# Graph attention on one core: feature transposes first in TensorE's turn, q[dst]·k last on VectorE, logits transposed one step earlier

## The chip, the cores and the metric

The kernel runs on one core of one Trainium2 chip. The metric is device time in microseconds (us), from start to end of one launch; the median over runs counts, and lower is better. Engines: PE (TensorE), DVE (VectorE), ACT (ScalarE), POOL (GpSimd), SP (SyncE, which issues most DMAs).

## The reference

One layer of graph attention over N = 12500 nodes and E = 212500 edges, sorted by destination, with 128 features in 8 heads of 16:

```python
h = jnp.maximum(_layernorm(x, axis=-1), 0.0)
q = (h @ Wq.T + bq).reshape(N, 8, 16)
k = (edge_attr @ Wk.T + bk).reshape(-1, 8, 16)
v = (h @ Wv.T + bv).reshape(N, 8, 16)
qs, qd = q[src], q[dst]
in_m   = sum(qs * k, -1)
out_m  = sum(qd * k, -1)
diag_m = sum(qs * qd, -1)
score = (segment_softmax(in_m * SCALE, dst) + segment_softmax(out_m * SCALE, dst)
         + segment_softmax(diag_m * SCALE, dst)) * distance ** lam
out = segment_sum(score[..., None] * v[dst], dst).reshape(N, 128) @ Wo.T + bo
return x + leaky_relu(out, 0.1)
```

So each edge needs three products of rows (q[src]·k, q[dst]·k, q[src]·q[dst]), each summed within 8 heads: 24 logits an edge, then a softmax over the edges of a node.

## The kernel before

**Steps and turns.** The edges lie in 415 blocks of 512 (4 columns of 128 edges). A block is a step g of the loop at L1586. Five steps (s = 0 to 4) make a turn t; there are 83 turns. The five blocks of a turn lie far apart in the list, so that their scans run side by side on 120 partitions (5 blocks × 24 logits).

**What a step does**, in the order in which the loop's body issues it:

- `gather(g + 18)` (L683): four indirect DMAs by POOL fetch q[src] for a block 18 steps ahead into one of 20 buffers `qq`.
- `spread_q(g + 1)`: four matmuls in bf16 (L1229) turn a window of q rows (`win`) and one-hot columns (`oh`) into q[dst], in PSUM `qd_ps` (2 buffers); ACT copies it to SBUF `qd` (L1232, 2 buffers).
- `project(g + 1)`: a bias matmul (L1219) and four fp32 matmuls (L1221, eight records in the trace) make k from the transposed features `eT`, in PSUM `k_ps` (2 buffers).
- `turn(g + 2)`: four transposes (L1212) of the edge features `ea` into PSUM `eT_ps` (one buffer); ACT copies that to `eT` (L1214, 3 buffers).
- `logits(g)`: DVE makes three products into `prod` (one buffer): qd·k (L1240), qq·qd_ps (L1241), qq·k (L1242), and reduces them by heads (L1243) into `lT`.
- `one_hots(g + 3)`: ACT makes the columns `oh` (L1206, L1207).

**What a turn does besides**, by its step s, for turns whose logits are complete:

- s = 0: `turn_logits(t - 2)` transposes `lT` into PSUM `l_ps` (L1263), `turn_head(t - 1)` transposes the next turn's first 64 edges into `h_ps` (L1271); DVE scans `l_ps` forwards in place (L1303) and copies its last column (`carry`, L1306), then scans the head (L1311, L1314).
- s = 1: DVE scans back (L1333) to the maximum of each node.
- s = 2: `turn_max` transposes the maxima (`m_ps`, L1345); DVE subtracts (L1353), ACT takes the exponential (L1354).
- s = 3: `show_ends` makes selection matrices on PE (`d_ps`, L1379) and ACT (`sel`, L1382, L1383); DVE weighs (L1365).
- s = 4: `to_rows` sums the edges into rows of nodes on PE (`w_ps`, L1393); ACT copies them (L1398), SP stores them.

These small PSUM tiles (`l_ps`, `h_ps`, `m_ps`, `d_ps`, `w_ps` and those of the node work mixed in) share three buffers.

**What sets the order.** Every engine runs its instructions in the order in which the code issues them: `pin` chains each instruction to the one before it on its engine, so an instruction that waits holds up all behind it. Between engines, semaphores follow the data. One order more is written out: `behind[g + 1, j]` names the PE instruction issued last at four points of a step, and the j-th gather of the next step's `gather` waits for it, besides waiting for its buffer `qq` to be free and for the gather before it:

```python
                if (g - LOOK, j) in behind:
                    tc.add_manual_dep(rows.ins, behind[g - LOOK, j], mybir.DependencyInfo(
                        mybir.DependencyClass.Sync, mybir.DependencyReason.SCHED_ONLY),
                        reason="close behind the products")
```

So PE's order in a step is: spread, project, transposes, then the small product of that s; the four gathers of the next step are opened by these four, in this order. PE's waits before: the spread for DVE's L1241 two steps back (it frees `qd_ps`), the bias for L1242 two steps back (it frees `k_ps`), the k product for ACT's copy `eT` of its own block. The transposes wait for nothing that the product before them hasn't waited for.

Of the kernel before, what the change touches and what calls it, by code (L numbers as in the profile page):

```python
# [472 lines left out]
def ordered_path(ctx: ExitStack, tc: tile.TileContext, flag, x, src, dst, edge_attr, edge_weight,  # L473
# [19 lines left out]
    nc = tc.nc  # L493
# [9 lines left out]
    G = T - 1  # L503
# [51 lines left out]
    pinned = {}  # L555

    def pin(inst):

        engine = str(inst.ins.engine)
        if engine in pinned:  # L560
            tc.add_manual_dep(inst.ins, pinned[engine], mybir.DependencyInfo(
                mybir.DependencyClass.NoSync, mybir.DependencyReason.DATA), reason="in order")
        pinned[engine] = inst.ins.name
        return inst
# [57 lines left out]
    end = S * G  # L622
# [11 lines left out]
    qqs, st, eas, behind, base_v = {}, {}, {}, {}, {}  # L634
# [33 lines left out]
    def fetch_edges(t):  # L668
        if t < G:
            ea = eas[t] = load.tile([P, S, JN * F], F32, name="ea")  # L670
            pin(nc.sync.dma_start(
                ea, edge_attr[:end * BE, :].rearrange("(s b p j) f -> p s b (j f)", s=S, b=G, p=P)
                [:, :, t, :]))
# [3 lines left out]
    def gather(g):  # L677
        if g < end:
            qq = firsts[g] if g < FIRST else gath.tile([P, JN, F], F32, name="qq")
            s, t = g % S, g // S  # L680
            for j in range(JN):
                of, at = (x, raw["i"][t]) if g < RAW else (q_table, src_i)
                rows = pin(nc.gpsimd.indirect_dma_start(  # L683
                    out=qq[:, j, :], out_offset=None, in_=of,
                    in_offset=bass.IndirectOffsetOnAxis(
                        ap=at[:, s, j:j + 1] if g < RAW else at[:, s * G + t, j:j + 1], axis=0)))
# [4 lines that stand above are left out]
            qqs[g] = qq  # L691
# [32 lines left out]
    with tc.tile_pool(name="prep", bufs=1) as prep, \  # L724
# [294 lines left out]
        for g in range(RAW):  # L1019
            turn = 1 + 2 * g if g < 4 else GN + g - 5  # L1020
# [81 lines left out]
    class Nodes:  # L1102
# [39 lines left out]
        def turn(self, to):  # L1142
            for b in range(self.n):
                pin(nc.tensor.transpose(to[:, b, :], self.h[:, b, :], ident))
            if self.hT is None:
                self.hT = fin.tile([P, JN, P], F32, name="hT")
            pin(nc.scalar.copy(self.hT[:, :self.n], to[:, :self.n]))
# [48 lines left out]
    with tc.tile_pool(name="work", bufs=2) as work, \  # L1196
            tc.tile_pool(name="scan", bufs=2) as scan, \
            tc.tile_pool(name="ps", bufs=1, space=PSUM) as ps:
        ks, eTs, qds, q_ps, ohs, lTs = {}, {}, {}, {}, {}, {}

        def one_hots(g):

            if g < end:
                oh = ohs[g] = work.tile([K3, BE], BF, name="oh", bufs=5)
                d = st[g // S]["relb"][:, g % S, :]
                pin(nc.scalar.activation(d, d, AF.Abs, bias=before[:K3]))  # L1206
                pin(nc.scalar.activation(oh, d, AF.Relu, bias=1.0, scale=-1.0))  # L1207
# [9 lines left out]
        def project(g):  # L1217
            k_ps = ks[g] = ps.tile([P, JN, F], F32, name="k_ps", bufs=2)
            pin(nc.tensor.matmul(k_ps, ones3, bk3, start=True, stop=False))  # L1219
            for j in range(JN):  # L1220
                pin(nc.tensor.matmul(k_ps[:, j, :], eTs[g][:, j, :], wk, start=False,  # L1221
                                     stop=(j == JN - 1)))
            del eTs[g]

        def spread_q(g):
            s, d = g % S, st[g // S]
            qd_ps = q_ps[g] = ps.tile([P, JN, F], F32, name="qd_ps", bufs=2)
            for j in range(JN):
                pin(nc.tensor.matmul(qd_ps[:, j, :], ohs[g][:, j * P:(j + 1) * P],  # L1229
                                     d["win"][:, s, :], start=(j == 0), stop=(j == JN - 1)))  # L1230
            qds[g] = work.tile([P, JN, F], F32, name="qd")
            pin(nc.scalar.copy(qds[g], qd_ps))  # L1232
            del ohs[g]

        def logits(g):
            s, t = g % S, g // S
            if s == 0:
                lTs[t] = scan.tile([P, JN, S, H3], F32, name="lT", bufs=4)
            prod = work.tile([P, JN, 3, F], F32, name="prod", bufs=1)
            pin(nc.vector.tensor_mul(prod[:, :, 2, :], qds[g], ks[g]))  # L1240
            pin(nc.vector.tensor_mul(prod[:, :, 1, :], qqs[g], q_ps[g]))  # L1241
            pin(nc.vector.tensor_mul(prod[:, :, 0, :], qqs[g], ks[g]))  # L1242
            pin(nc.vector.tensor_reduce(lTs[t][:, :, s, :],  # L1243
                                        prod.rearrange("p j i (h d) -> p j (i h) d", d=DIM), AX.X,
                                        ALU.add))
            del ks[g], qds[g], q_ps[g], qqs[g]
# [121 lines left out]
        def select(t):  # L1368
            at, part = block_rows(t)
            ends = ends_t[t % 2 if t < G - 1 else t - G + 3]  # L1370
            pin(nc.sync.dma_start(ends[1:, :], rel_d[part].rearrange("(s b) (j p) -> s b j p", b=G, j=JN)
                                  [:, at, :, :]))
# [42 lines left out]
        def later(f, t, *more):  # L1415
            if 0 <= t < T:
                f(t, *more)

        def nodes_before(t, s):

            new, old = pairs.get(t - t % 2), pairs.get(t - t % 2 - 2)
            if new and t % 2 == 1 and s == 4:
                new.project_v(small([P, JN, F], "node_ps"))
            if old and t % 2 == 0 and s == 4:
                old.project_o(small([P, JN, F], "node_ps"))
# [155 lines left out]
        products = str(mybir.EngineType.PE)  # L1581
# [9 lines left out]
        for g in range(end):  # L1591
            s, t = g % S, g // S
            nodes_before(t, s)
            if g >= FIRST:
                gather(g + LOOK)
            if s == 0:
                fetch_edges(t + 1)
            if g + 1 < end:
                spread_q(g + 1)
                behind[g + 1, 0] = pinned[products]  # L1600
                project(g + 1)
                behind[g + 1, 1] = pinned[products]
            if g + 2 < end:
                turn(g + 2)
                behind[g + 1, 2] = pinned[products]
            logits(g)
            one_hots(g + 3)
            if s == 0:
                later(turn_logits, t - 2)
                later(turn_head, t - 1)  # L1610
                later(scan_here, t - 2)
                if t > 1:
                    scan_head(t - 1)
                later(select, t - 2)
            elif s == 1:
                later(scan_back, t - 2)
                if t == 1:
                    logits_few()
            elif s == 2:
                later(turn_max, t - 2)  # L1620
                later(powers, t - 2)
                if t == G - 1:
                    turn_logits(t - 1)
                    scan_on(t - 1)
            elif s == 3:
                later(show_ends, t - 2)
                later(weigh_powers, t - 2)
                fetch(t + 2)
            else:
                later(to_rows, t - 2)  # L1630
            ahead, k = (t + 2, s - 3) if s > 2 else (t + 1, s + 2)
            if ahead > 1:
                fetch_rows(ahead, [k])
            later(put_rows, t - 2 if s == 4 else t - 3, [(s + 1) % S])
            if t == G - 1:
                if 0 < s < 4:
                    select(G - 3 + s)
                elif s == 4:
                    for i in (G - 2, G - 1, G):
                        show_ends(i)  # L1640
            behind[g + 1, 3] = pinned[products]
            nodes_between(t, s)
            terms_between(t, s)
            if g == 4:
                show_places()
            elif g == 7:
                show()
            elif 0 <= g - 21 < len(tests):
                tests[g - 21]()
            begin_rest(g - (end - DRAIN))  # L1650
            if g < S:
                of = [u for u in range(NU) if g in parts_of(u)]
                pin(nc.scalar.dma_start(
                    sums[g][of[0] * UN:(of[0] + len(of)) * UN].rearrange(
                        "(n p) i c -> p n (i c)", p=P),
                    blank[:, None, :].to_broadcast([P, 2 * len(of), 2 * 2 * H3])))
# [97 lines left out]
```

## Time and profile before

| | |
|---|---|
| median of 3 runs | 2754.93 us (2752.01 to 2763.2) |
| profiled execution | 2753.89 us |
| its span, first to last instruction | 2752.0 us |
| granted TensorE clock, mean | 0.763 |
| DMA, read and written | 320.86 MB, 32.17 MB |
| loop in its steady part, 300 to 2580 us | 379 reduces, 1516 gathers |
| busy there | PE 1589.71, DVE 1773.01, ACT 1145.24, POOL 1440.12 us |

How to read the lines of groups: line of code, engine, operation, output<-inputs, shapes, count | busy us in all, mean ns of one | idle us of that engine just before them, and what ended most of it. "remote" and "issue" stand for waits whose releaser the profile doesn't name. In a timeline the first two numbers are the start and the duration, and a bracket holds the idle time ahead and its releaser. PE's groups of matmuls are shown as one row each, and their ends are modelled.

### The profile page before, as it was taken

What the parts mean: (1) busy time and instruction counts of PE and PEld (TensorE: products, weight loads), DVE (VectorE), ACT (ScalarE), POOL (GpSimd) and SP (SyncE); (2) the same over time, 40 slices, a digit from 0 to 9 for tenths busy, and PEclk for the clock granted to TensorE, in tenths of its full rate; (3) what the DMA queues carried; (4) which work ended last, traced back from release to release, by engine and by line L of the source; (5) the groups of instructions that cost most, each with busy time, mean ns of one, the idle gap of its engine ahead of it and who ended that gap; (6) DMA issues with size and microseconds to landing.
All of it is one profiled execution on the core that took longest, in us unless ns stands there. A gap on an engine that the chain in (4) does not pass through costs nothing.

```text
span 2752.0 us, 36272 instructions
## 1 busy us (share of the span) xinstructions
PE 1869.1 (68%) x10744; PEld 1495.9 (54%) x10744; DVE 2061.8 (75%) x2844; ACT 1370.8 (50%) x2518; POOL 1595.9 (58%) x1683
## 2 busy tenths in 40 slices
PE   2736666666677767666767767676667776776786
PEld 1624555555555655555556556555555565655664
DVE  3636787777787877877878777777877778778894
ACT  2734545444455545554555445455444554555572
POOL 6244666666666666666666666666666666666400
PEclk9867777877777778788787777777877777777786
DMA  6247444444454454444434444444444444344321
GB/s 185 84 135 219 119 134 121 133 136 125 127 153 140 124 151 135 128 149 124 125 121 138 128 121 121 140 127 121 123 136 120 118 143 134 110 137 130 116 88 51
DMA packets 321411, 355.65 MB, mean 129 GB/s; under 512 B 135266, under 2 KB 241005, under 8 KB 320896
## 3 DMA queue, kind: packets, MB, share of 16 engines
q1 hardware_dynamic: 250853, 237.91, 27.3%
q0 software_dynamic: 53184, 108.92, 15.7%
q10 hardware_dynamic: 17168, 6.41, 1.0%
q8 instruction: 88, 1.44, 0.2%
q14 instruction: 118, 0.97, 0.1%
HBM read 320.86 MB, written 32.17 MB: 128 GB/s over the span
## 4 chain that ended last, share of the span: by engine, by line
PE 37%; DVE 18%; ACT 15%; another core or an unknown queue 14%; issue 13%; DMA 1%; SPq 1%; ACTq 1%; DVEq 0%; POOL 0%; POOLq 0%
PE k_ps L1221 12%; PE w_ps L1393 7%; PE eT_ps L1212 5%; DVE lT L1243 4%; PE qd_ps L1229 4%; ACT eT L1214 3%; PE k_ps L1219 3%; DVE prod L1240 2%; DVE prod L1241 2%; DVE l_ps L1303 2%; ACT relb L1206 2%; ACT oh L1207 2%; DVE prod L1242 2%; ACT qd L1232 2%
## 5 line engine op out<-in xcount | busy, mean ns | idle before, releaser
L683 POOL DMA_INDIRECT qq<-q_table,src_i x1608 | 1528.9, 951 | 940.0 <-issue 323.3
L1221 PE MATMUL k_ps<-wk,eT 128*128 128x128 f32 x3320 | 655.9, 358 | 508.2 <-issue 261.5
L1221 PEld LDWEIGHTS k_ps<-wk,eT 128*128 128x128 f32 x3320 | 555.9, 253 | 661.9 <-issue 356.8
L1243 DVE TENSOR_REDUCE lT<-prod 128x96 f32<-128x1536 f32 x415 | 727.5, 1753 | 14.4
L1214 ACT COPY eT<-eT_ps 128x512 f32<-128x512 f32 x415 | 244.4, 589 | 785.1 <-remote 539.4
L1240 DVE TENSOR_TENSOR prod<-qd,k_ps 128x512 f32<-128x512 f32 x415 | 281.1, 677 | 197.1 <-remote 134.2
L1232 ACT COPY qd<-qd_ps 128x512 f32<-128x512 f32 x415 | 240.7, 580 | 229.5 <-PE qd_ps L1229 72.7
L1212 PE MATMUL eT_ps<-ident,ea 128*128 128x128 f32 x1660 | 342.8, 345 | 0.9 <-DVE qq L992 0.9
L1229 PE MATMUL qd_ps<-win,oh 126*128 126x128 bf16 x1660 | 186.5, 243 | 171.0 <-DVE prod L1241 82.6
L1206 ACT ACTIVATE relb<-relb,before 126x512 bf16<-126x512 bf16 x415 | 302.4, 729 | 0.0
L1242 DVE TENSOR_TENSOR prod<-qq,k_ps 128x512 f32<-128x512 f32 x412 | 280.3, 680 | 0.0
L1241 DVE TENSOR_TENSOR prod<-qq,qd_ps 128x512 f32<-128x512 f32 x412 | 280.1, 680 | 0.0
L1212 PEld LDWEIGHTS eT_ps<-ident,ea 128*128 128x128 f32 x1660 | 276.0, 185 | 1.1 <-DVE qq L992 1.1
L1207 ACT ACTIVATE oh<-relb 126x512 bf16<-126x512 bf16 x415 | 262.1, 632 | 15.3 <-DMA q_table<-q3o 2.2
L1229 PEld LDWEIGHTS <-oh 126*128 126x128 bf16 x1660 | 139.4, 110 | 230.3 <-issue 215.9
L1393 PE MATMUL w_ps<-back,sel 128*126 128x144 f32 (+1 forms) x1344 | 239.9, 343 | 25.5 <-ACT sel L1383 6.3
L1393 PEld LDWEIGHTS w_ps<-back,sel 128*126 128x126 f32 (+1 forms) x1344 | 222.0, 238 | 52.6 <-ACT sel L1383 34.7
L1303 DVE TENSOR_TENSOR_SCAN l_ps<-far,carry,l_ps 120x512 f32<-120x512 bf16 x80 | 103.0, 1288 | 187.4 <-remote 65.0
L1219 PE MATMUL k_ps<-b,ones 3*128 3x512 bf16 x415 | 178.5, 430 | 18.6 <-DVE prod L1242 11.2
L1333 DVE TENSOR_TENSOR_SCAN m<-far,head,l_ps 120x512 f32<-120x512 bf16 x81 | 103.0, 1272 | 0.0
L1398 ACT COPY rows<-w_ps 126x288 f32<-126x288 f32 x84 | 33.1, 395 | 134.1 <-PE l_ps L1263 35.1
L1353 DVE TENSOR_TENSOR back<-lT,m_ps 128x480 f32<-128x480 f32 x83 | 54.1, 652 | 54.0 <-PE m_ps L1345 16.2
(230 smaller groups left out, 1697.4 us busy)
## 6 DMA issues: line engine op xcount, KB each, us to landing
ea<-in_edge_attr_dram SPq DMA_DIRECT2D x83, 1280.0 KB
relb<-rel_d SPq DMA_DIRECT2D x83, 630.0 KB
qq<-q_table,src_i POOLq DMA_INDIRECT x1608
win<-q_table SPq DMA_DIRECT2D x415, 31.5 KB
far<-far_d SPq DMA_DIRECT2D x84, 120.2 KB
q_table<-q SPq DMA_DIRECT2D x18, 384.0 KB
sums<-rows SPq DMA_DIRECT2D x412, 7.9 KB
q_table<-xq SPq DMA_DIRECT2D x24, 256.0 KB
```

The lines of the kernel that those rows point to most:

```text
L683: rows = pin(nc.gpsimd.indirect_dma_start(out=qq[:, j, :], out_offset=None, in_=of, in_offset=bass.IndirectOffsetOnAxis(ap=at[:, s, j:j + ...
L1206: pin(nc.scalar.activation(d, d, AF.Abs, bias=before[:K3]))
L1207: pin(nc.scalar.activation(oh, d, AF.Relu, bias=1.0, scale=-1.0))
L1212: pin(nc.tensor.transpose(eT_ps[:, j, :], eas[g // S][:, g % S, j * F:(j + 1) * F], ident))
L1214: pin(nc.scalar.copy(eT, eT_ps))
L1221: pin(nc.tensor.matmul(k_ps[:, j, :], eTs[g][:, j, :], wk, start=False, stop=(j == JN - 1)))
L1229: pin(nc.tensor.matmul(qd_ps[:, j, :], ohs[g][:, j * P:(j + 1) * P], d["win"][:, s, :], start=(j == 0), stop=(j == JN - 1)))
L1240: pin(nc.vector.tensor_mul(prod[:, :, 2, :], qds[g], ks[g]))
L1241: pin(nc.vector.tensor_mul(prod[:, :, 1, :], qqs[g], q_ps[g]))
L1242: pin(nc.vector.tensor_mul(prod[:, :, 0, :], qqs[g], ks[g]))
L1243: pin(nc.vector.tensor_reduce(lTs[t][:, :, s, :], prod.rearrange("p j i (h d) -> p j (i h) d", d=DIM), AX.X, ALU.add))
L1393: pin(nc.tensor.matmul(w_ps[:, i].rearrange("p s c -> p (s c)"), d["sel"][:n, j, lo:lo + 3, :].rearrange("p s w -> p (s w)"), d["back"][:n ...
```

## The change

Three things move; no instruction is added or taken away on any engine.

1. In the loop, `turn(g + 2)` goes ahead of `spread_q(g + 1)` and `project(g + 1)`. The points that open the gathers are renamed in the new order: the first gather of the next step follows the transposes, the second the spread, the third the project, the fourth the small product, as before.
2. In `logits`, the product of q[dst] and k (into `prod[:, :, 2]`) moves from first to last; qq·q[dst] is now first and qq·k second.
3. `turn_logits` of a turn moves from step s = 0 to the step before it, s = 4 of the turn before, behind `to_rows`.

PE's order in a step is then: transposes, spread, project, small product. The transposes of g + 2 now come before the k product of g + 1, and wait for ACT's copy of the transposes of g + 1, since `eT_ps` has one buffer; the k product has no wait of its own left. The spread waits for DVE's first product two steps back, as it is the one that reads `qd_ps`. DVE's first product needs `qd_ps` and `qq`, the second `k_ps`, the third ACT's copy `qd`. The small PSUM tiles are handed out in the same order as before.

```diff
@@ logits
             prod = work.tile([P, JN, 3, F], F32, name="prod", bufs=1)
-            pin(nc.vector.tensor_mul(prod[:, :, 2, :], qds[g], ks[g]))
             pin(nc.vector.tensor_mul(prod[:, :, 1, :], qqs[g], q_ps[g]))
             pin(nc.vector.tensor_mul(prod[:, :, 0, :], qqs[g], ks[g]))
+            pin(nc.vector.tensor_mul(prod[:, :, 2, :], qds[g], ks[g]))
@@ the loop
+            if g + 2 < end:
+                turn(g + 2)
+                behind[g + 1, 0] = pinned[products]
             if g + 1 < end:
                 spread_q(g + 1)
-                behind[g + 1, 0] = pinned[products]
+                behind[g + 1, 1] = pinned[products]
                 project(g + 1)
-                behind[g + 1, 1] = pinned[products]
-            if g + 2 < end:
-                turn(g + 2)
                 behind[g + 1, 2] = pinned[products]
             logits(g)
             one_hots(g + 3)
             if s == 0:
-                later(turn_logits, t - 2)
                 later(turn_head, t - 1)
...
             else:
                 later(to_rows, t - 2)
+                if t < G - 1:
+                    later(turn_logits, t - 1)
```

## The prediction

> **What bounds the kernel now.** I read the page's totals first, then the groups of lines over the steady loop (300 to 2580 us), the waits there, one timeline, and the groups again over 2610 to 2680 us, where no gathers run.
>
> ```profile
> PE 1869.1 (68%) x10744; PEld 1495.9 (54%) x10744; DVE 2061.8 (75%) x2844; ACT 1370.8 (50%) x2518; POOL 1595.9 (58%) x1683
> ...
> PE 37%; DVE 18%; ACT 15%; another core or an unknown queue 14%; issue 13%; DMA 1%; SPq 1%; ACTq 1%; DVEq 0%; POOL 0%; POOLq 0%
> ```
>
> No engine is full, and 27% of the chain is waits without a named owner (14% + 13%). The loop shows where they sit:
>
> ```profile
> L683 POOL DMA_INDIRECT qq<-q_table,src_i x1516 | 1441.2, 951 | 840.0 <-issue 301.1 <-remote 244.7 <-PE qd_ps L1229 80.4
> L1243 DVE TENSOR_REDUCE lT<-prod 128x96 f32<-128x1536 f32 x379 | 664.4, 1753 | 13.1
> L1221 PE MATMUL k_ps<-wk,eT 128*128 128x128 f32 x3032 | 600.7, 359 | 487.6 <-issue 257.9 <-ACT eT L1214 227.4 <-ACT qd L1232 1.8
> ...
> L1214 ACT COPY eT<-eT_ps 128x512 f32<-128x512 f32 x378 | 222.7, 589 | 744.9 <-remote 529.2 <-PE qd_ps L1229 115.4 <-PE eT_ps L1212 62.8
> ...
> L1229 PE MATMUL qd_ps<-win,oh 126*128 126x128 bf16 x1516 | 170.0, 243 | 154.6 <-DVE prod L1241 76.1 <-issue 43.6 <-DVE prod L1240 25.0
> ...
> L1303 DVE TENSOR_TENSOR_SCAN l_ps<-far,carry,l_ps 120x512 f32<-120x512 bf16 x76 | 97.9, 1288 | 186.7 <-remote 65.0 <-PE qd_ps L1229 29.6 <-PE h_ps L1271 26.9
> ```
>
> 379 reduces in 2280 us make 6.02 us a step, though DVE needs 1773.0 us there and PE 1589.7. Next to PE's own work, its largest idle time is 487.6 us ahead of the product with k, for ACT's copy of eT; and that copy stood 744.9 us, 529.2 of them behind nothing named. The timeline shows why:
>
> ```profile
> 1509.00 0.60 PE L1212 MATMUL eT_ps<-ident,ea 128*128 128x128 f32 x4
> ...
> 1513.08 0.38 PE L1229 MATMUL qd_ps<-win,oh 126*128 126x128 bf16 x4 [3.04 <-DVE prod L1241]
> ...
> 1515.68 0.59 ACT L1214 COPY eT<-eT_ps 128x512 f32<-128x512 f32 x1 [5.32 <-remote]
> ...
> 1516.32 2.07 PE L1221 MATMUL k_ps<-wk,eT 128*128 128x128 f32 x8 [2.27 <-issue]
> ```
>
> The transposes end at 1509.60; the idle ACT copies 6.08 us later, 1.66 us after POOL's gather that ran from 1513.07 to 1514.02. PE's word reaches ACT late, often only in POOL's pauses. Without gathers the same lines read:
>
> ```profile
> L1243 DVE TENSOR_REDUCE lT<-prod 128x96 f32<-128x1536 f32 x15 | 26.3, 1753 | 0.5
> L1221 PE MATMUL k_ps<-wk,eT 128*128 128x128 f32 x112 | 19.6, 328 | 0.1
> ```
>
> 15 reduces in 70 us are 4.67 us a step, and PE's wait is 0.1. So two things set the pace together: POOL's gathers (0.95 busy + 0.30 between = 1.25 us; 1516 take 1895 of the 2280 us, leaving 385 us of pauses, of which I counted 258 over 0.5 us, so 5.9 gathers a run), and PE, whose progress opens the gathers and which stands for late copies.
>
> **The change part by part.** (a) Work: the same instructions on every engine; 0 us. SP's queue keeps its order. POOL issues the same gathers; their four gates, before spread, project, transposes, small product, are now transposes, spread, project, small product. In a circle that is PE's same order, so they open at the same spacing: 0 us. The first gather of a step also waits for the last product that reads its old buffer; this is now the second instead of the third, 0.60 us earlier, counted under (d).
>
> (b) Slack for eT. Before, between transposes of g+1 and their use lie the small product, the spread (170.0/379 = 0.45 us) and the bias (162.9/379 = 0.43). Now the k product (600.7/379 = 1.58) lies between as well, so each stall ahead of k can shrink by up to 1.58. Counted in the loop's timeline: 185 stalls, of which 1.58 or less each gives 243.5 us (130 are longer and keep a rest). That is PE time, not the end's. Two ways to carry it over: PE spends 1589.7/1516 = 1.05 us on each gather's share, so a pause filled with 243.5/258 = 0.94 us more PE work opens about 0.9 gathers, runs grow from 5.9 to 6.8, the pause of 1.49 us (385/258) is spread over more, and a gather costs 1.25 + 1.49/6.8 = 1.469 us instead of 1.503: 1516 × 0.034 = 51 us. Or from the loop itself: over 70 turns I regressed a turn's length on its stalls; a us of k stall costs 0.34 us, one of qd stall 0.58. 243.5 × 0.34 = 82. I take the middle, **-66**; bounds 0 (POOL's runs unchanged) and -243.
>
> (c) The new wait. Transposes of g+2 now wait for the copy of g+1, as eT_ps is one buffer, and spread, project and small queue behind them; DVE and the gathers wait for these. Cover is 0.45 + 0.43 + 1.58 = 2.46 us plus the small product, against a copy of 0.589 plus the lateness; where it suffices, 0. Where a late word comes at POOL's pause whatever PE did, k now follows by transposes (313.8/379 = 0.83), spread and bias: 1.71 us later than before. If that holds for all 130 long stalls: 130 × 1.71 × 0.34 = 76. I take a quarter, as a run usually ends when PE's gates are exhausted, so moves with PE: **+19**; bounds 0 and 76.
>
> The Trainium skill ("Perfetto Trace Analysis", Optimizing Tensor Performance, Matmuls) wants independent matmul groups rotated through PSUM banks so that one's evacuation overlaps the next's matmuls; this single eT_ps, refilled at the head of the turn, speaks against the change. By the rule each step would pay the copy, 0.589 × 415 = 244 us more; by the rows above other products lie between. No run here shows it yet.
>
> (d) Order of the products. qq·q[dst] goes first (needs no k and no copy of q[dst]); it frees qd_ps 0.60 us earlier (start to start, timeline). 78 qd stalls, the first 0.6 of each: 48 us × 0.58 = 28 at most; k becomes first need of the second product, and DVE's 176.8 us ahead of its first product moves there or shrinks. The q[dst] copy is freed 1.2 us later, under the reduce of 1.753; if that cover is gone, ACT's copy is late, and eT's copy, queued behind it, with it. I take **-10**; bounds -28 and, for the copy, at 78 stalls (1.2 less the spread's 0.45) × 0.34 = +20.
>
> (e) l_ps one step earlier. The scan's 186.7 us over 76 turns moves to the head scan, which still needs h_ps; only the scan and carry, 1.288 + 0.16 = 1.45 us a turn, can run before that: counted, 96.9 us, at 0.13 us per us (same regression, scan wait) = 13. PE's l_ps is the same 46.4 us, now in s=4 behind w_ps, where a gather gate moves 0.61 us later. **-4**; bounds -13 and +8 (76 × 0.61 × 0.17, half the k rate).
>
> Sum: -66 + 19 - 10 - 4 = -61. The profiled execution took 2753.89 us (span 2752.0 and 1.9 around it), 1.0 under the median of 2754.93. 2755 - 61 = **2694**.
>
> **The clock.** PE's clock falls after stalls: the k product takes 1.16 us at 1508.01 and 2.07 at 1516.32; the loop's mean is 0.76, and 0.85 without gathers. Fewer stalls could raise it; I count it in the low bound only. The skill's "TensorE: Matmul & The Clock Gate", Why this matters for your kernels, says gaps over about 3 us throw the clock back to half, and this row's 2.27 us stall behind a 3.04 one fits; by it, shortening the 130 longest stalls under 3 us would give back some of the 0.9 us each.
>
> **Rivals.** 1. *Larger gain* (15%): the lateness follows PE, nearly all of the 243.5 lands on runs of 8 gathers or more: 1.25 + 1.49/8 = 1.436 us, -101, and half of the loop's clock loss on k (0.9 us × 130 / 2 × 0.34 = 20), so 2634. For: 4.67 us a step is possible. Against: POOL's 1895 us remain.
> 2. *No change* (13%): a run is what PE opened since the last pause, and each pause lets one copy of eT through, so PE gets one set of transposes further, in either order; runs stay 5.9, (b) and (c) are 0, and half of (d) and (e), which hang on PE's word too, gives -7: 2748. For: copies bunch 1.5 to 2.2 us after a run's last gather. Against: one step opens 4 gathers, and most runs have 5 to 8.
> 3. *Slower* (25%): the blocked transposes. The word comes at POOL's pause, so all 185 stalls stay as long, and k follows each by 1.71: 185 × 1.71 × 0.34 = +108, less 20 for (d) and (e): 2843. Between it and (b) it decides from 243.5/1.71 = 142 of 185 stalls that are fixed by POOL; at 160 of them, (160 - 142) × 1.71 × 0.34 = +10. Middle of this case 2800. For: the shown copy came with the pause. Against: the median lateness of PE's word, which I counted at 2.2 to 2.7 us, is inside the new cover.
>
> **How the numbers follow.** The forecast has 47%; with rival 1 that is 0.62 for faster by over 0.5% (14 us, about what a measurement can tell from no change), 0.13 within, 0.25 slower. The forecast's own range is 2655 to 2735 ((b) from -51 to -82, (c) from 0 to 76, the others' bounds). For 8 in 10 I reach past rival 1's 2634 (with the full bounds of (d) and (e), -41 in place of -14, 2607; I take 2600) and to 2815, just past the middle of the slower case; about a tenth lies beyond, and a little below.
>
> **What would show it.** Idle before k (487.6) should fall under 260 and reappear, smaller, before the transposes L1212 (0.0 now); POOL's idle before gathers (840.0) falls by some 60; scan L1303's 186.7 goes to about 90, with L1311 taking it. If idle before L1212 grows beyond what k lost, rival 3 is right; if POOL's 840.0 stands, rival 2. I am wrong in the step of 0.34 if k's stall falls as said and the time doesn't.

## The result and the profile after

The changed kernel takes 2749.57 us (2742.29 to 2757.73, 20 runs) against 2756.01 us before: a ratio of 0.9973, 95% interval [0.9965, 0.9981]. That is 0.27% faster, within the 0.5% (14 us) that the prediction took as no change; 2694 was forecast, so 6.4 us were gained where 61 were expected. The kernel before takes 2719 to 2756 us on most chips but 2205 to 2208 us on three others, so every ratio below is against the kernel before on the same chip, and which of the two a chip was is said where it matters.

The totals of the page and the chain of waits:

```profile
PE 1943.1 (71%) x10744; PEld 1545.6 (56%) x10744; DVE 2061.8 (75%) x2844; ACT 1376.1 (50%) x2518; POOL 1589.6 (58%) x1683
...
PE 39%; DVE 16%; issue 9%; ACT 9%; another core or an unknown queue 7%; DMA 2%; DVEq 1%; SPq 1%; POOL 0%; ACTq 0%; POOLq 0%
```

The groups of lines in the steady loop, 300 to 2580 us (busy us, mean ns | idle us ahead of them and its releasers):

```profile
L683 POOL DMA_INDIRECT qq<-q_table,src_i x1518 | 1436.1, 946 | 845.9 <-issue 310.4 <-remote 218.2 <-PE qd_ps L1229 99.7
L1243 DVE TENSOR_REDUCE lT<-prod 128x96 f32<-128x1536 f32 x379 | 664.3, 1753 | 13.1
L1221 PE MATMUL k_ps<-wk,eT 128*128 128x128 f32 x3032 | 574.7, 345 | 10.0 <-issue 9.8
...
L1212 PE MATMUL eT_ps<-ident,ea 128*128 128x128 f32 x1518 | 314.2, 343 | 260.7 <-issue 180.4 <-ACT eT L1214 57.3 <-DMA ea<-in_edge_attr_dram 6.5
...
L1393 PE MATMUL w_ps<-back,sel 128*126 128x144 f32 x1201 | 265.5, 401 | 158.3 <-ACT sel L1383 144.7 <-issue 8.4 <-ACT sel L1382 2.8
L1241 DVE TENSOR_TENSOR prod<-qq,k_ps 128x512 f32<-128x512 f32 x379 | 258.1, 681 | 208.1 <-remote 129.1 <-PE k_ps L1221 38.6 <-PE eT_ps L1212 10.1
...
L1214 ACT COPY eT<-eT_ps 128x512 f32<-128x512 f32 x379 | 219.7, 580 | 329.1 <-remote 171.5 <-PE qd_ps L1229 26.3 <-PE k_ps L1221 25.4
L1229 PE MATMUL qd_ps<-win,oh 126*128 126x128 bf16 x1516 | 186.1, 256 | 27.7 <-DVE prod L1240 17.2 <-issue 10.1 <-DMA win<-q_table 0.2
...
L1303 DVE TENSOR_TENSOR_SCAN l_ps<-far,carry,l_ps 120x512 f32<-120x512 bf16 x76 | 97.5, 1282 | 16.0 <-PE l_ps L1263 6.4 <-PE qd_ps L1229 6.2 <-PE eT_ps L1212 2.2
...
L1345 PE MATMUL m_ps<-ident,m 120*128 120x120 f32 x304 | 70.6, 374 | 102.8 <-issue 54.2 <-DVE prod L1241 21.7 <-ACT hT L1147 15.8
```

Rows of the kernel before in the same window:

```profile
L1212 PE MATMUL eT_ps<-ident,ea 128*128 128x128 f32 x1516 | 313.8, 346 | 0.0
...
L1393 PE MATMUL w_ps<-back,sel 128*126 128x144 f32 x1207 | 215.0, 342 | 20.8 <-issue 4.8 <-ACT sel L1383 4.8 <-ACT sel L1382 2.9
...
L1345 PE MATMUL m_ps<-ident,m 120*128 120x120 f32 x304 | 71.8, 386 | 1.9 <-DVE m L1333 1.5 <-issue 0.4
```

The change did what it was to do at its place: idle time ahead of the k product went from 487.6 to 10.0 us, ahead of the spread from 154.6 to 27.7, ahead of the scan from 186.7 to 16.0. Yet 379 reduces in 2280 us are what they were. What went away came back on other lines: 260.7 us ahead of the transposes (0.0 before), 158.3 ahead of w_ps (20.8), 102.8 ahead of m_ps (1.9), 208.1 ahead of DVE's second product (0.0; ahead of its first it was 176.8 and is 97.9). POOL's row is the one that didn't move: 845.9 us idle, 840.0 before. The busy times of each engine in the same window, before and then after (columns PE, PEld, DVE, ACT, POOL, then PE's clock, DMA share and GB/s), show where PE's saved waiting went:

```profile
300.00:2580.00 2280.00, 1589.71 (x9223) 1274.66 (x9222) 1773.01 (x2241) 1145.24 (x2047) 1440.12 (x1516) 0.76 0.45 131
...
300.00:2580.00 2280.00, 1671.12 (x9227) 1328.22 (x9225) 1776.20 (x2245) 1153.29 (x2050) 1434.39 (x1518) 0.73 0.44 131
```

PE is busy 1671.1 us instead of 1589.7: 81 us more for the same matmuls, at a clock of 0.73 instead of 0.76; its idle time fell by the same 81. What PE saved in waiting it spent in slower matmuls.

### The profile page after: what moved, and what is told of

Read it like the earlier page. It is cut to its first block, busy times and chain, and to the rows that moved or that the text cites. A ratio compares the mean times of both kernels' runs of the same rounds, so it can differ in the third digit from the quotient of the medians.

```text
span 2745.6 us, 36004 instructions
## 1 busy us (share of the span) xinstructions
PE 1943.1 (71%) x10744; PEld 1545.6 (56%) x10744; DVE 2061.8 (75%) x2844; ACT 1376.1 (50%) x2518; POOL 1589.6 (58%) x1683
## 4 chain that ended last, share of the span: by engine, by line
PE 39%; DVE 16%; issue 9%; ACT 9%; another core or an unknown queue 7%; DMA 2%; DVEq 1%; SPq 1%; POOL 0%; ACTq 0%; POOLq 0%
PE k_ps L1221 11%; PE w_ps L1393 7%; PE eT_ps L1212 6%; DVE lT L1243 4%; PE qd_ps L1229 3%; PE k_ps L1219 3%; DVE prod L1241 2%; DVE prod L1240 2%; DVE prod L1242 2%; PE node_ps L1152 2%; PE m_ps L1345 2%; ACT sel L1382 1%; ACT relb L1206 1%; PE d_ps L1379 1%
## 5 line engine op out<-in xcount | busy, mean ns | idle before, releaser
L1243 DVE TENSOR_REDUCE lT<-prod 128x96 f32<-128x1536 f32 x415 | 727.4, 1753 | 14.3
L1221 PE MATMUL k_ps<-wk,eT 128*128 128x128 f32 x3320 | 627.5, 345 | 10.0 <-issue 9.8
L1221 PEld LDWEIGHTS k_ps<-wk,eT 128*128 128x128 f32 x3320 | 529.0, 241 | 169.0 <-issue 168.2
L1212 PEld LDWEIGHTS eT_ps<-ident,ea 128*128 128x128 f32 x1660 | 244.1, 176 | 354.5 <-issue 232.0
L1393 PE MATMUL w_ps<-back,sel 128*126 128x144 f32 (+1 forms) x1344 | 287.9, 393 | 162.7 <-ACT sel L1383 147.5
L1393 PEld LDWEIGHTS w_ps<-back,sel 128*126 128x126 f32 (+1 forms) x1344 | 268.5, 280 | 179.0 <-ACT sel L1383 161.0
L1229 PEld LDWEIGHTS <-oh 126*128 126x128 bf16 x1660 | 162.2, 118 | 58.2 <-issue 43.8
L1345 PE MATMUL m_ps<-ident,m 120*128 120x120 f32 x332 | 77.4, 376 | 108.9 <-issue 55.6
L1382 ACT ACTIVATE sel<-d_ps 128x420 f32<-128x420 f32 x168 | 78.3, 513 | 149.6 <-remote 99.4
L1354 ACT ACTIVATE back<-back 128x480 f32<-128x480 f32 x83 | 50.0, 603 | 186.0 <-DVE back L1353 139.0
L1345 PEld LDWEIGHTS m_ps<-ident,m 120*128 120x128 f32 x332 | 55.3, 217 | 124.4 <-issue 69.0
```

Of the source, the lines that this page charges most:

```text
L1212: pin(nc.tensor.transpose(eT_ps[:, j, :], eas[g // S][:, g % S, j * F:(j + 1) * F], ident))
L1243: pin(nc.vector.tensor_reduce(lTs[t][:, :, s, :], prod.rearrange("p j i (h d) -> p j (i h) d", d=DIM), AX.X, ALU.add))
L1393: pin(nc.tensor.matmul(w_ps[:, i].rearrange("p s c -> p (s c)"), d["sel"][:n, j, lo:lo + 3, :].rearrange("p s w -> p (s w)"), d["back"][:n ...
```

## The experiments

Twelve kernels ran besides these two, some of them more than once, eighteen runs in all, in seven sets, each set on one chip with the kernel before beside it. "us a gather" is a stretch of the loop divided by its gathers. As every step of these kernels has four gathers, it is a quarter of a step's time and no measurement of its own, and it differs from chip to chip as the times do. "gathers a run" counts those between POOL's pauses of over 0.5 us idle.

| kernel | us | ratio to before | us a gather | gathers a run |
|---|---|---|---|---|
| before | 2756.0 | 1 | 1.504 | 5.9 |
| changed | 2749.6 | 0.9973 [0.9965, 0.9981] | 1.502 | 5.5 |
| turn_first | 2710.4 | 0.9973 [0.9957, 0.9990] | 1.480 | 5.8 |
| product_last | 2719.2 | 0.9998 [0.9988, 1.0009] | 1.486 | 6.2 |
| logits_early | 2713.3 | 0.9983 [0.9971, 0.9994] | 1.483 | 6.1 |
| word_more | 2710.8 | 0.9977 [0.9965, 0.9988] | 1.481 | 5.9 |
| word_kept | 2766.0 | 1.0171 [1.0151, 1.0190] | 1.520 | 5.6 |
| word_less | 2720.5 | 0.9999 [0.9990, 1.0009] | 1.487 | 6.4 |
| ungated | 2964.3 | 1.0798 [1.0780, 1.0816] | 1.641 | 8.5 |
| pairs | 2751.1 | 1.0031 [1.0015, 1.0047] | 1.501 | 7.9 |
| turn_twice_3 | 2758.1 | 1.0026 [1.0015, 1.0038] | 1.512 | 5.0 |
| two_eT_2 | 2801.6 | 1.0188 [1.0165, 1.0211] | 1.529 | 4.9 |

The kernel before took 2718.7 us beside turn_first, product_last, logits_early and word_more, 2719.4 beside the two word kernels, 2744.1 beside ungated and pairs, 2752.5 beside the last two.

**Each part alone.** Does one part give back what another brings?

```diff
# turn_first: the kernel before, and
+            if g + 2 < end:
+                turn(g + 2)
+                behind[g + 1, 0] = pinned[products]
             if g + 1 < end:
                 spread_q(g + 1)
...
# product_last: the kernel before, and
-            pin(nc.vector.tensor_mul(prod[:, :, 2, :], qds[g], ks[g]))
...
+            pin(nc.vector.tensor_mul(prod[:, :, 2, :], qds[g], ks[g]))
# logits_early: the kernel before, and
-                later(turn_logits, t - 2)
...
+                if t < G - 1:
+                    later(turn_logits, t - 1)
```

> The kernel before with only the first of the three moves: transposes first in PE's turn, gates renamed. Theory 'parts cancel': this part alone brings what was forecast for it, -47 us (ratio about 0.983), and another part gives it back. Theory 'words' (a turn takes as long as PE needs to get its finished-work signals out between POOL's gathers, about 4 of them in each pause, and their number is unchanged): within 0.5% of the kernel before, idle time moves from before k (487.6 us in the loop) to other lines of PE.

> The kernel before with only the second move: q[dst]*k last on DVE. 'Parts cancel': either -10 as forecast, or slower by up to 40 us, if this is the part that gives the gain back. 'Words': within 0.5%.

> The kernel before with only the third move: l_ps one step earlier, behind w_ps. 'Parts cancel': -4 as forecast, or slower by up to 40 us, since PE's stretch in s = 4 grows by 0.61 us and the wait before w_ps went from 20.8 to 158.3 us in the changed kernel. 'Words': within 0.5%.

No part measured more than 0.3%, and all three are at or below 1, so no part gives back what another brings. Turning first alone has the ratio of the whole change, and moves PE's waits in the same way (300 to 2540 us):

```profile
L1221 PE MATMUL k_ps<-wk,eT 128*128 128x128 f32 x3024 | 581.4, 348 | 20.7 <-issue 20.5
L1212 PE MATMUL eT_ps<-ident,ea 128*128 128x128 f32 x1516 | 312.3, 342 | 206.2 <-issue 148.0 <-ACT eT L1214 51.4 <-ACT back L1354 3.6
```

product_last and logits_early show shifts of the same kind, in the lines of 300 to 2540 us, first of the one, then of the other:

```profile
L1221 PE MATMUL k_ps<-wk,eT 128*128 128x128 f32 x3016 | 596.3, 359 | 435.7 <-issue 254.9 <-ACT eT L1214 170.9 <-ACT qd L1232 9.3
...
L1241 DVE TENSOR_TENSOR prod<-qq,k_ps 128x512 f32<-128x512 f32 x376 | 256.2, 681 | 84.6 <-remote 61.0 <-PE qd_ps L1229 22.6 <-PE node_ps L1152 0.9
...
L1240 DVE TENSOR_TENSOR prod<-qq,qd_ps 128x512 f32<-128x512 f32 x376 | 255.1, 678 | 43.1 <-issue 14.7 <-ACT qd L1232 12.4 <-ACT sel L1383 8.1
```

```profile
L1221 PE MATMUL k_ps<-wk,eT 128*128 128x128 f32 x3016 | 595.3, 358 | 554.4 <-ACT eT L1214 321.2 <-issue 227.0 <-ACT qd L1232 5.7
...
L1303 DVE TENSOR_TENSOR_SCAN l_ps<-far,carry,l_ps 120x512 f32<-120x512 bf16 x76 | 97.6, 1284 | 36.9 <-PE qd_ps L1229 16.2 <-PE eT_ps L1212 9.0 <-PE k_ps L1221 6.8
...
L1311 DVE TENSOR_TENSOR_SCAN u_head<-far,carry,h_ps 120x64 f32<-120x64 bf16 x76 | 26.4, 347 | 45.5 <-remote 30.5 <-PE eT_ps L1212 5.4 <-PE qd_ps L1229 3.4
```

DVE's wait ahead of its first products shrank from 176.8 us to 43.1 + 84.6, with no time gained. The scan's wait fell from 186.7 to 36.9 us, the head scan's rose from 9.6 to 45.5, and PE's ahead of k from 487.6 to 554.4. (The values before are of the kernel before on the first chip, where it took 2754 us, in a window 40 us longer.)

**Is it the number of PE's signals?** Three variants of the changed kernel; `halfway` is the second of the four transposes, and `close` makes an instruction wait for the k product's last matmul as well.

```diff
# word_more
-                behind[g + 1, 0] = pinned[products]
+                behind[g + 1, 0] = halfway[g + 2]
# word_kept: ACT's copy of q[dst] and DVE's first product wait for the k product
-            pin(nc.scalar.copy(qds[g], qd_ps))
...
+            close(pin(nc.scalar.copy(qds[g], q_ps[g])), g)
# word_less: word_kept, and
+                project(g + 1)
                 behind[g + 1, 1] = pinned[products]
-                project(g + 1)
                 behind[g + 1, 2] = pinned[products]
```

> The changed kernel, with the first gather of a step gated by the second of the four transposes instead of the last. PE's work is the same and the gate opens earlier, but PE must signal twice in the transposes: 2472 signals from PE instead of 2078. 'Words': +394 signals / 3.7 for each pause x 1.49 us = +159 us (ratio about 1.058); at least +60 us. Rivals, in which PE's work, its clock or the gates' order set the time: -10 to +10 us.

> The changed kernel, in which ACT's copy of q[dst] and DVE's first product wait for the product with k that follows the spread, not for the spread itself. The second gather of a step is still gated by the spread, so PE still signals there: 2066 signals. All theories: same or slower, 0 to +40 us (1.58 + 0.43 us later for the copy and the first product). It is the control for the next run.

> As the run before, with the second gather gated by the product with k as well, so that PE has no signal to give behind most spreads: 1751 signals instead of 2066, and a gate that opens about 2 us later. 'Words': 315 fewer / 3.7 for each pause x 1.49 us = -127 us against the control (ratio about 0.95); at least -50. Rivals: the later gate makes it slower or does nothing, 0 to +40 us against the control.

394 signals more cost nothing (0.9977, the whole change 0.9973), so their number doesn't set the time: the theory of "words" fell as it was put. word_kept is 1.7% slower: a copy and a product that wait 2 us longer do cost. word_less is 46 us faster than its control, about a third of the 127 expected; but it changes the signal and the second gather's gate together, so which of the two did it stays open.

**Do the gates or the length of POOL's runs set the pace?** Two more variants of the changed kernel.

```diff
# ungated
-                if (g - LOOK, j) in behind:
-                    tc.add_manual_dep(rows.ins, behind[g - LOOK, j], mybir.DependencyInfo(
...
# pairs
-                if (g - LOOK, j) in behind:
-                    tc.add_manual_dep(rows.ins, behind[g - LOOK, j], mybir.DependencyInfo(
+                if g % 2 == 0 and (g - LOOK, 2) in behind:
+                    tc.add_manual_dep(rows.ins, behind[g - LOOK, 2], mybir.DependencyInfo(
```

> The changed kernel with no gates on the gathers: each waits only for its buffer, which DVE's products of two steps before free. DVE's signals are not held back. 'Pauses': gathers come as soon as DVE frees them, four a step, so pauses are set by DVE and PE's signals still come late: within 2% of the changed kernel, either way. 'Gates set the pace' (gathers come too late because PE opens them): 60 us or more faster.

> The changed kernel with gates for two steps at a time: the four gathers of even steps wait for the k product of the step before, those of odd steps for nothing but their buffers, so that POOL gets eight at once. 'Pauses': runs become 8 instead of 5.5, so 8 x 1.25 + 1.49 = 11.5 us for two steps instead of 12.04: -100 us if PE and DVE keep up behind held signals, or slower if they don't. 'PE's path': within 0.5%.

pairs is the run that tells most. POOL's row of 300 to 2100 us:

```profile
L683 POOL DMA_INDIRECT qq<-q_table,src_i x1199 | 1136.6, 948 | 665.3 <-issue 295.1 <-remote 184.1 <-PE k_ps L1221 58.5
```

1199 gathers in 1800 us are 1.501 us each, although the runs are eight long (147 of 151), so what 'Pauses' expected, 100 us less, didn't come. The pauses grew with the runs: 1800 - 1199 × 1.25 = 301 us over 151 pauses is 2.0 us each beyond the usual spacing, against 1.49 before. The same shows within the kernel before when its pauses, counted in the same way, are sorted by the run ahead of them: about 1.2 us after five gathers, 1.5 after six, 1.9 after eight; in the changed kernel 1.25, 1.4 and 1.7. After a run of a single gather it is 1.1 in both, so the pause grows with the run but not in proportion to it. What a longer run saves in the number of pauses it pays, here, in their length. Over any 20 gathers in a row the mean is 1.505 us in the kernel before and 1.504 in the changed one, with a standard deviation of 0.03 in both. Without gates it is worse: runs of 8.5 and pauses of 3.3 us, 8% slower, which neither theory had.

**Half of the gathers; the transposes done twice; a second eT_ps buffer.**

```diff
# half_before, half_after
+            if g > 40 and g % 2:
+                qqs[g] = qqs[g - 1]
+                return
# turn_twice: the changed kernel, and
-            for j in range(JN):
+            for j in [*range(JN), *range(JN)]:
                 pin(nc.tensor.transpose(eT_ps[:, j, :], eas[g // S][:, g % S, j * F:(j + 1) * F], ident))
# two_eT: the changed kernel, and
-            eT_ps = ps.tile([P, JN, P], F32, name="eT_ps", bufs=1)
+            eT_ps = ps.tile([P, JN, P], F32, name="eT_ps", bufs=2)
...
-            return ps.tile(shape, F32, name=name, tag="small", bufs=3)
+            return ps.tile(shape, F32, name=name, tag="small", bufs=2)
...
-            of.held = ps.tile([P, JN, F], F32, name=name, bufs=1 if name == "eT_ps" else 2)
+            of.held = ps.tile([P, JN, F], F32, name=name, bufs=2)
```

> The kernel before with half of the gathers: from step 41 on, odd steps take the rows of q[src] that the even step before fetched (so those logits use other rows). Theory 'pauses' (PE's signals are held back while a run of gathers is going, and come out some 1.8 us after it; the time is 25 us of gathers a turn plus the pauses, whatever PE's order): from 6.02 to 4.7 to 5.2 us a step, so 2350 to 2460 us. Theory 'PE's path' (PE's chain with its waits and its clock sets the pace, gathers are beside it): under 3% faster.

> The changed kernel with the same half of the gathers. 'Pauses': the same drop, within 1% of the half kernel without the change if the waits for late signals are gone; the forecast's own reasoning (slack for the copy is worth up to 1.58 us a stall) gives at most as much as stalls before k are left there. 'PE's path': under 3% faster than the changed kernel.

> The changed kernel with the four transposes of a step done twice, the second time over the first result: PE's work grows by 0.83 us a step, 344 us in all, with no other signal or wait. 'Pauses': PE's idle 609 us of the loop takes most of it, 0 to +100 us. 'PE's path': +200 to +344 us (ratio 1.07 to 1.13).

> The changed kernel with two PSUM buffers for eT_ps and two instead of three for the small products: the transposes no longer wait for ACT's copy of the step before. 'Pauses': within 1% of the changed kernel, as idle time before the transposes (260.7 us in the loop) moves to other lines. 'PE's path', or the new wait as the one that gave the gain back: 60 to 120 us faster; slower only if the third small buffer was needed.

On that chip the kernel before took 2207.7 us. half_before took 2199.8 (0.9963 [0.9949, 0.9977]), half_after 2187.7 (0.9904 [0.9887, 0.9920]), turn_twice 2205.8 (0.9992 [0.9982, 1.0001]), two_eT 2224.4 (1.0073 [1.0056, 1.0090]). A step of half_before is 4.79 us there, and half of the gathers, left out, saves only 0.4%. So none of the four spoke to the 2750 us, and they ran again.

> The kernel before with half of the gathers (odd steps from 41 on take the rows of the even step before), on a chip on which the kernel before takes over 2700 us. On the chip of the first try it took 2208 us whole and 2200 with half, PE's signals were not late, and POOL stood in one unbroken run of 1.25 us a gather. 'Held signals': here the halves bring 300 us or more, towards 2200 to 2400, since gathers are what holds PE's signals. 'The chip's own slowness' (signals late whatever POOL does): under 100 us.

> The changed kernel with half of the gathers. 'Held signals': with twice the time between runs of gathers, slack decides again: 10 to 60 us below the half kernel without the change. 'The change is worth nothing where signals are late': within 0.5% of it.

> The changed kernel with the transposes done twice (PE +0.83 us a step, 344 us in all), which cost nothing where PE's signals were on time. 'Held signals': PE's idle time takes it here too, 0 to +60 us. 'PE's path, slowed by its clock, sets the pace where PE stalls': +150 us or more.

Again the kernel before took 2204.7 us: half_before_2 0.9975 [0.9964, 0.9985], half_after_2 0.9931 [0.9914, 0.9948], turn_twice_2 0.9996 [0.9984, 1.0008]. The next set found the other kind of chip, 2752.5 us:

> The changed kernel with the transposes done twice (PE +0.83 us a step, 344 us in all), hoped for on a chip where the kernel before takes over 2700 us; on two chips where it takes 2205 to 2208 us this cost nothing. 'Held signals': PE's idle time takes it, -10 to +60 us. 'PE's path, slowed by its clock, sets the pace where PE stalls': +150 us or more.

> The changed kernel with two PSUM buffers for eT_ps and two for the small products, on the same chip as the run above. 'Held signals': the wait before the transposes (260.7 us) goes and comes back on other lines, within 1% of the kernel before. 'The new wait gave the gain back': 40 to 120 us faster. Where signals were on time it was 0.7% slower, the price of the third small buffer.

So the same program, turn_twice, has a profile of both kinds. On the chip of turn_twice_2, the totals and the chain, then POOL and the transposes of 300 to 2580 us (its loop ends earlier, hence fewer gathers in the window):

```profile
PE 1838.1 (84%) x12404; PEld 1516.6 (69%) x12404; DVE 2043.0 (93%) x2844; ACT 1362.2 (62%) x2518; POOL 1594.7 (72%) x1683
...
DVE 41%; PE 22%; DMA 11%; issue 4%; ACT 4%; POOL 2%; DVEq 1%; SPq 0%; ACTq 0%; POOLq 0%
```

```profile
L683 POOL DMA_INDIRECT qq<-q_table,src_i x1462 | 1387.2, 949 | 445.6 <-issue 194.8 <-DMA qq<-q_table,src_i 117.0 <-PE eT_ps L1212 26.5
...
L1212 PE MATMUL eT_ps<-ident,ea 128*128 128x128 f32 x3040 | 461.5, 302 | 24.3 <-ACT eT L1214 24.2
```

And on the chip of turn_twice_3:

```profile
PE 2052.8 (74%) x12404; PEld 1683.3 (61%) x12404; DVE 2064.5 (75%) x2844; ACT 1377.1 (50%) x2518; POOL 1590.6 (58%) x1683
...
PE 57%; issue 13%; DVE 10%; ACT 9%; another core or an unknown queue 7%; DMA 1%; DVEq 1%; ACTq 1%; SPq 0%; POOL 0%; POOLq 0%
```

```profile
L683 POOL DMA_INDIRECT qq<-q_table,src_i x1508 | 1428.1, 947 | 852.7 <-issue 294.4 <-remote 195.9 <-PE qd_ps L1229 105.9
...
L1212 PE MATMUL eT_ps<-ident,ea 128*128 128x128 f32 x3016 | 513.7, 325 | 331.2 <-issue 273.4 <-ACT eT L1214 44.8 <-ACT hT L1147 4.9
```

A gather takes POOL the same 0.95 us in both. In the first, gathers follow one another every 1.253 us without a pause from 300 us to their end at 2132, and DVE is 93% busy. Where ACT stood idle, its copy of eT started 0.04 us in the median after the transposes had ended and ACT was free. As neither half of the gathers nor the transposes done twice moved the time there by 1%, DVE mostly sets it; four gathers take 5.01 us to a step of 4.78, and the lead of 18 steps covers the rest, though not always: the gathers' DMA is 11% of the chain. In the second a gather comes every 1.51 us, and the same delay of ACT's copy is 2.0 us.

On that second chip the transposes done twice made the time 0.26% longer than before; against the changed kernel's ratio that is 1.0026/0.9973, or +15 us. The added work was meant to be 344 us, but by what PE stood busy it is less, as its clock rose with it:

```profile
300.00:2580.00 2280.00, 1755.39 (x10700) 1441.31 (x10697) 1766.72 (x2232) 1147.90 (x2040) 1427.61 (x1508) 0.80 0.44 130
```

PE is busy 84 us more than in the changed kernel in this window (1755.4 against 1671.1) and 110 us more in the whole execution (2052.8 against 1943.1), at a clock of 0.80 instead of 0.73. So most of PE's added busy time, some 95 of 110 us, cost nothing; that 344 us would have cost as little isn't shown.

two_eT_2 takes away the transposes' new wait, and is slower:

```profile
L1212 PE MATMUL eT_ps<-ident,ea 128*128 128x128 f32 x1492 | 294.8, 331 | 15.5 <-remote 10.5 <-issue 4.8
...
L1229 PE MATMUL qd_ps<-win,oh 126*128 126x128 bf16 x1492 | 178.7, 252 | 59.6 <-issue 32.3 <-DVE prod L1240 10.1 <-DVE prod L1241 5.5
...
L1345 PE MATMUL m_ps<-ident,m 120*128 120x120 f32 x296 | 69.5, 376 | 123.6 <-issue 45.2 <-ACT hT L1147 43.9 <-DVE m L1333 23.2
```

The 260.7 us ahead of the transposes are down to 15.5, and others rise: PE's idle time in the window is 683 us, 609 in the changed kernel. The Trainium skill ("Perfetto Trace Analysis", Optimizing Tensor Performance, Matmuls) would have groups rotate through banks, as this run does; measured, it is 1.9% slower, and 0.7% where signals are on time. The buffer came from the small products, so this run changes two things: that the lost third small buffer is the price is likely and not shown, and what a second eT_ps would bring without it stays open.

The last run tried half of the gathers a third time:

> The kernel before with half of the gathers, a third time, alone. If the kernel before takes over 2700 us beside it: 'held signals' expects 300 us or more off, towards 2200 to 2400, as half the gathers hold PE's signals half as long; 'the chip's own slowness' expects under 100 us off. If the kernel before takes about 2205 us again, the state is bound to which programs are on the chip together or to chance, and half of the gathers again gives less than 1%.

The kernel before took 2206.3 us beside it, and half_before_3 2197.3 (0.9955 [0.9938, 0.9971]). So what half of the gathers does where signals are late was never measured. All three sets that met the 2205 us began with a kernel of half the gathers, on three different chips; the four other sets, on four other chips, didn't. Whether that is chance or cause these runs don't tell.

## Why the prediction was wrong

**Right: where the loop stood.** PE stood ahead of k for late copies of eT, behind signals that reach ACT late. The k stall fell below 260 us, the wait came back ahead of the transposes, and the scan's wait fell below 90, more than forecast.

**Wrong: (b), the carry-over.** The step that failed is "a pause filled with 243.5/258 = 0.94 us more PE work opens about 0.9 gathers, runs grow from 5.9 to 6.8, the pause of 1.49 us (385/258) is spread over more". Runs did not grow: 274 pauses of 1.40 us beyond the usual spacing stand in place of 258 of 1.49, 5.5 gathers a run, and POOL's idle time stayed (845.9 us, 840.0 before). Where runs were made to grow, in pairs, to 7.9, the pause grew to 2.0 us: it is no constant that longer runs spread. The other way to the same number, the 0.34 us of a turn for each us of k stall, fell with it: the stalls ahead of k and of the spread lost 604 us in the loop (642.2 to 37.7), and the loop's length stayed. That slope compared turns among themselves, in which a long stall and a long turn may both follow from late signals, and it hangs on where a turn is cut: in the same loop of the kernel before, a regression on the waits of k, spread and scan gives 0.06 us for a us of k stall with turns cut at DVE's first reduce, 0.10 at POOL's gathers, 0.35 at the transposes of the maxima (m_ps) and 0.46 at PE's first transposes. So it was no price of a stall. Turning first alone, forecast at -47 with its new wait, gave 0.9973.

**(c), the new wait,** was right in kind. It holds 260.7 us of PE's time. Without it the kernel isn't faster (two_eT_2), though a small buffer is missing there too; so that it did not eat up the gain is likely rather than shown. Its +19 rests on the slope of 0.34, and no run shows it.

**(d), the order of the products,** forecast at -10 us, ratio 0.9964, measured 0.9998 [0.9988, 1.0009]: nothing. **(e), the logits,** forecast at -4, measured 0.9983 [0.9971, 0.9994] of 2718.7, -5 us: right in size.

**(a)** the gates' renaming was rightly put at nothing, so far as the whole change is near nothing; it wasn't run alone.

**The clock.** Counted as a possible gain, it went the other way: 0.735 from 0.763. The stalls ahead of k were 175 over 0.35 us; now 119 stand ahead of the transposes, 54 ahead of w_ps and 59 ahead of m_ps. PE's stalls of over 3 us, which the prediction hoped to shorten, fell from 97 to 70 in the loop, and the clock fell all the same. Nor does the number of stalls tell it: product_last has 95 over 0.35 us in 100 steps at a clock of 0.76, the changed kernel 87 at 0.73. In turn_twice_3, where PE has more to do, it is 0.794. Why it fell isn't shown.

**The rivals.** *No change* (13%, 2748 us) is what came, 2749.57. Its sign, POOL's idle 840.0 standing still, was the one seen, and it was right that PE's order does not alter what POOL's runs and pauses take together. Its picture of one eT for each pause isn't shown, and runs went from 5.9 to 5.5. That the number is so near is partly luck: its -7 us came from (d) and (e), with nothing from (b), but turning first alone measured -7 us (0.9973). *Slower* by blocked transposes did not come: it supposed that the stalls stay as long and that k follows, and k's went; and it counted PE's delay at the same 0.34. *Larger gain* fell with (b).

**The range.** The forecast's own range, 2655 to 2735, is narrower than the bounds it names: -82 to -51, 0 to 76, -28 to +20 and -13 to +8 add up to 2632 to 2808, in which 2749.57 lies. And rival 3 takes off 20 us for (d) and (e), where the sum has 14; that moves it by 6.

What stays open is why a gather costs 1.50 us where signals are late. That PE's signals wait behind something that the gathers fill, and that drains more slowly than POOL fills it, would fit pauses that grow with the run, but no run shows it. Nor is it shown why the time stayed when PE's stalls moved, beyond that they came back on other lines.

## What to carry to other kernels

A stall that an in-order engine loses at one wait comes back at the next, unless that wait's cause is gone; before counting it as time, add work to that engine, read from its busy time how much was added, and see whether the time moves. A slope between stalls and lengths of the same loop's turns is no price; cut the turns elsewhere and see whether it holds. When two engines feed each other, as POOL's runs and pauses and PE's signals do here, don't hold one factor (the pause) fixed while moving the other (the run).

## What the runs showed of the hardware that was not expected

- The same program (turn_twice) took 2203.5 us on one chip and 2758.1 on another: on the first ACT's copy of eT, where ACT stood idle, started 0.04 us in the median after the transposes had ended and ACT was free, on the second 2.0 us, though a reduce took 1753 ns on both and a gather 949 and 947.
- Where signals are late, a gather takes about 1.50 us with its share of the pauses, almost whatever the order of the work: eleven gated kernels lie between 1.480 and 1.529, the one without gates at 1.641. Where they are on time it is 1.253, with a deviation of 0.007 over any 20 in a row.
- Where PE's signals are late, ACT's and DVE's are not: in the kernel before PE's k product started 0.05 us after ACT's copy of eT whenever it waited for it (182 times, 167 of them within a run of gathers), and in the changed one ACT's exponential 0.03 us after DVE's subtraction (70 times). PE's recorded signals come at 0.45 to an interval between gathers without a pause in the kernel before, and at 3.7 in a pause.
